# A list scheduler gets measured issue and landing times for transfers through DRAM

## The chip, the cores and the metric

The kernel runs on one NeuronCore of one Trainium2 chip. The metric is the device time of one execution in microseconds (us). A profile is one further execution, recorded by the hardware profiler; its span runs from its first to its last instruction. Engines are named as in the profile: PE (matmuls), PEld (weight loads), DVE (vector), ACT (scalar), POOL (GpSimd), SP (the engine that issues nearly all DMAs here).

## The reference, cut to what matters

Sixteen graphs (x is 16 x 1024 x 128) share one symmetric 0/1 adjacency matrix of 1024 x 1024. Layer 0 is an attention layer, layer 1 a gated graph network with five steps, and each is followed by a residual and a layernorm.

```python
h = x @ others_weight
e = leaky_relu(u1[:, idx1] + u2[:, idx2])        # u1 = h @ a1, u2 = h @ a2
att = softmax(where(adj > 0, e, NEG_BIG), axis=1)
x = layernorm(x + att @ h + x @ self_weight)
h = x
for _ in range(5):                               # per graph
    m = adj @ h                                  # in_matrix and out_matrix are both adj
    av = concat([m, m])
    u3 = h @ u3_w.T + u3_b
    z = sigmoid(av @ w3_w.T + w3_b + u3)
    r = sigmoid(av @ w4_w.T + w4_b + u3)
    hv = tanh(av @ w5_w.T + w5_b + (r * h) @ u5_w.T + u5_b)
    h = (1 - z) * h + z * hv
x = layernorm(x + h)
```

## The kernel before

One graph is called a batch b. Its state h lives turned, as hT (128 features x 1024 nodes), in two halves of 512 nodes. Per step s (`step`), PE makes m = adj @ h in two halves, each 16 matmuls at line 878: eight blocks of 128 nodes, each with a high and a low part of h (hN), since hN and adj are kept in fp32r. ACT copies each half out (line 896). Then per half: u from u3 (PE 908, ACT 911), the sums and gates r and z (PE 918, DVE 921, ACT 924), r times h (DVE 932), the candidate (PE 938 and 939, ACT 942), and three DVE operations that update hT (949, 956, 963). The gates' matmuls are plain fp32. For the next step h must be turned back, node by feature, and split into the high part (ACT cast, line 497) and the low part (DVE, line 501), together hN.

The turning is done by `flip` in most steps: a DVE transpose in blocks of 32 x 32 into tile T (line 478), then four DMA issues that write T to a DRAM tile D with blocks swapped (`away`, line 483), then one DMA issue that reads D back to tile F (line 487). Here it is called a flip. Layer 0 flips its result y and the normalised y (tiles T_y, D_y, F_y and T_b, D_b, F_b). `on_pe` makes the first two batches' layer-0 turns, and the last three batches' last step's, on PE instead (line 468, into PSUM). Layer 0 (`layer0`) also loads xt (line 516), and for b of 2 and more sends 24 rows (us) to DRAM as ud (line 573), from which come pb, spread over all partitions (line 580), and uu (line 587). A layernorm is bn_stats on DVE (441, 443), a power on POOL (447 to 450) and scaling on ACT (455). The result goes out at line 1006. Sixteen `look` loads of adj (line 1026) feed a late check.

The order of all this is not written by hand. Each operation is given to a planner, `Plan`, by `pe`, `dve`, `act`, `sp` and `plan.add`, with an engine, a length in ns, a rank (5b + 3s plus offsets from the table D; other spacings for the last two batches), and the values it reads and writes. `Plan.order` is a list scheduler: it runs a simulated clock, and whenever an engine is free it starts the ready operation of lowest rank whose tiles have a free buffer. Lengths on DVE and ACT are raised by 1.2. A user becomes ready at the end of the length plus a lag: LAG by the producer's engine, or SAME if the user is on the same engine:

```python
SAME = {"PE": 0, "DVE": 60, "ACT": 60, "POOL": 60, "SP": 2500, "DMA": 0}
LAG = {"PE": 250, "DVE": 150, "ACT": 170, "POOL": 200, "SP": 2500, "DMA": 2400}
```

So every DMA that SP issues was reckoned to land 2500 ns after its length. The order found is then emitted, and on the chip each engine's queue runs in that order[...]. An SP operation may hold several DMA issues: `away` has four, `uu_` two.

Of the kernel before, what the change touches and what calls it, by code (L numbers as in the profile page):

```python
# [30 lines left out]
class Plan:  # L31
# [11 lines left out]
    def __init__(self, slots):  # L43
        self.slots = dict(slots)
        self.ops = []
        self.writer, self.readers = {}, {}

    def add(self, engine, length, rank, emit, reads=(), writes=()):
        i = len(self.ops)
        deps = {self.writer[v] for v in reads if v in self.writer}  # L50
        for v in writes:
            deps |= self.readers.pop(v, set())
            if v in self.writer:
                deps.add(self.writer[v])
        for v in reads:
            self.readers.setdefault(v, set()).add(i)
        for v in writes:
            self.writer[v] = i
        deps.discard(i)
        tiles = {v[0] for v in (*reads, *writes) if v[0][0] in self.slots}  # L60
        if engine in ("DVE", "ACT"):
            length *= self.MARGIN
        self.ops.append((engine, length, rank, emit, deps, tiles))

    def order(self):
        ops, free = self.ops, dict(self.slots)
        users, left = [[] for _ in ops], []
        uses = {}
        for i, (_, _, _, _, deps, tiles) in enumerate(ops):
            left.append(len(deps))  # L70
            for d in deps:
                users[d].append(i)
            for t in tiles:
                uses[t] = uses.get(t, 0) + 1
        ready, busy, live = {}, {}, set()
        at = {}
        events = [(0, 0, i) for i in range(len(ops)) if not left[i]]
        heapq.heapify(events)
        started = []
        while events:  # L80
            now = events[0][0]
            while events and events[0][0] == now:
                _, what, i = heapq.heappop(events)
                engine, _, rank, _, _, tiles = ops[i]
                if what == 0:
                    heapq.heappush(ready.setdefault(engine, []), (rank, i))
                elif what == 1:
                    busy.pop(engine)
                    for t in tiles:
                        uses[t] -= 1  # L90
                        if not uses[t]:
                            free[t[0]] += 1
            more = True
            while more:
                more = False
                for engine, queue in ready.items():
                    if engine in busy:
                        continue
                    later = []
                    while queue:  # L100
                        rank, i = heapq.heappop(queue)
                        _, length, _, _, _, tiles = ops[i]
                        new = [t for t in tiles if t not in live]
                        if all(free[t[0]] > 0 for t in new):
                            for t in new:
                                free[t[0]] -= 1
                                live.add(t)
                            started.append(i)
                            busy[engine] = more = True
                            heapq.heappush(events, (now + length, 1, i))  # L110
                            for u in users[i]:
                                left[u] -= 1
                                lag = self.SAME[engine] if ops[u][0] == engine else self.LAG[engine]
                                at[u] = max(at.get(u, 0), now + length + lag)
                                if not left[u]:
                                    heapq.heappush(events, (at[u], 0, u))
                            break
                        later.append((rank, i))
                    for x in later:
                        heapq.heappush(queue, x)  # L120
        assert len(started) == len(ops)
        return started
# [3 lines left out]
def kernel(  # L126
# [52 lines left out]
    nc = tc.nc  # L179
# [26 lines left out]
    def exact(pools):  # L206
# [45 lines left out]
        def T(t, dtype=None, shape=None):  # L252
            if t not in tiles:
                _, sh, dt, _ = kinds[t[0]]
                tiles[t] = places[t[0]].tile(
                    shape or sh, dtype or dt, tag=t[0], name="_".join(map(str, t)).replace("-", "n")
                )
            return tiles[t]
# [25 lines left out]
        def sp(*a, **k):  # L284
            plan.add("SP", *a, **k)
# [31 lines left out]
        def early_loads():  # L317
# [28 lines left out]
            writes=[(boot, "early"), (ws, "early"), (x0, "early"), (("xt", 1), "early"), *((t, "early") for t in staged)],  # L346
# [125 lines left out]
        def flip(name, src, read, dst, write, rank):  # L472


            t, d = ("T", *name), ("D", *name)

            def turn():
                nc.vector.transpose(T(t).rearrange("p (b c i) -> p b c i", b=4, c=4), turned(src()))

            def away():  # L480
                swapped = T(d).rearrange("(b i) (a x) -> a i b x", b=4, a=4)
                for k in range(4):
                    nc.sync.dma_start(swapped[k], T(t)[32 * k : 32 * (k + 1), :].rearrange("i (b x) -> i b x", b=4))  # L483

            dve(V, rank, turn, reads=read, writes=[(t, 0)])
            sp(280, rank, away, reads=[(t, 0)], writes=[(d, 0)])
            sp(70, rank, lambda: nc.sync.dma_start(dst(), T(d)), reads=[(d, 0)], writes=[write])

        def split(b, s, g, src, read, rank):

# [16 lines left out]
        def layer0(b):  # L507

            first = rank_of(b, 0) - (60 if b == 0 else 0)
            rank = first + D["l1"]  # L510
            xt, hx, pb, u, us, uu, ud = (
                ("xt", b), ("hx", b), ("pb", b), ("u3", b), ("us", b), ("uu", b), ("ud", b)
            )
            q, zs, rz, yT, y0, hT = ("q", b), ("zs", b), ("rz", b), ("yT", b), ("y0", b), ("hT", b)
            if b >= 2:
                sp(2700, rank, lambda: nc.sync.dma_start(T(xt), x_t[b]), writes=[(xt, 0), (xt, 1)])

            for g in range(4):
                ph = ("ps", "g", b, "ph", g)
# [37 lines left out]
            if b >= 2:  # L557
# [6 lines left out]
                    reads=[(u, 0), (u, 1), (("ident",), 0)],  # L564
                    writes=[(put, 0)],
# [2 lines left out]
                    280, rank, lambda: nc.vector.tensor_copy(T(us), T(put)[0 : 3 * NC, 0:P]), reads=[(put, 0)], writes=[(us, 0)]  # L568
                )
                sp(  # L570
                    60,
                    rank,
                    lambda: nc.sync.dma_start(T(ud).rearrange("t (c p) -> (t c) p", p=P), T(us)),
                    reads=[(us, 0)],
                    writes=[(ud, 0)],
                )
                sp(
                    60,
                    rank,
                    lambda: nc.sync.dma_start(T(pb), T(ud)[2:3, :].to_broadcast([P, N])),  # L580
                    reads=[(ud, 0)],
                    writes=[(pb, 0), (pb, 1)],
                )

                def uu_():
                    for w in range(2):
                        nc.sync.dma_start(T(uu)[:, w, :], T(ud)[w].rearrange("(c p two) -> two p c", p=P, two=2)[w])

                sp(120, rank, uu_, reads=[(ud, 0)], writes=[(uu, 0)])

            else:

# [275 lines left out]
        def step(b, s):  # L868
# [99 lines left out]
            for g in range(2):  # L968
                gs = slice(4 * g, 4 * g + 4)
                o = ("o", b)  # L970

                def h(g=g):
                    return T(hT)[:, g * HALF : (g + 1) * HALF]

                if on_pe(b, s):
                    t = ("ps", "t", b, s, g)
                    transposes(h, [(hT, g)], t, rank + D["tr"])

                    def n(t=t):
                        return T(t).rearrange("p (c a j) -> p c a j", c=4, a=4)  # L980

                else:
                    t = ("F", b, s, g)
                    flip((b, s, g), h, [(hT, g)], lambda t=t: T(t), (t, 0), rank + D["tr"])

                    def n(t=t):
                        return chunks(T(t))

                if s < STEPS - 1:
                    split(b, s + 1, g, n, [(t, 0)], rank + D["split"])  # L990
                    continue

                def last(n=n, g=g, gs=gs):
                    dst = T(o)[:, gs, :].rearrange("p c (a j) -> p c a j", a=4)
                    nc.vector.tensor_tensor(dst, n(), T(y0)[:, gs, :].rearrange("p c (a j) -> p c a j", a=4), ALU.add)

                dve(V, rank + D["o"], last, reads=[(t, 0), (y0, g)], writes=[(o, "raw", g)])
                
                def at(j, g=g):
                    return T(o)[:, 4 * g + j, :]  # L1000

                layernorm(o, g, rank + D["ln"], (o, "raw", g), at, at, (o, g))
                sp(
                    60,
                    rank + D["out"],
                    lambda gs=gs: nc.sync.dma_start(
                        out[b].rearrange("(c p) d -> p c d", p=P)[:, gs, :], T(o)[:, gs, :]
                    ),
                    reads=[(o, g)],
                )  # L1010
# [332 lines left out]
```

## Time and profile before

| | us |
|---|---|
| three runs | 1522.34, 1528.13, 1528.56 (median 1528.13) |
| the profiled execution | 1530.39 |
| its span | 1528.60 |
| PE busy in it | 1497.9 (98%) |
| DVE, ACT, POOL busy | 1171.3, 841.6, 141.0 |
| mean granted PE clock | 0.993 |
| flips: D<-T, D_y<-T_y, D_b<-T_b issues | 616 + 112 + 112 |
| flips: F<-D, F_y<-D_y, F_b<-D_b issues | 154 + 28 + 28 |

The page gives, per engine, the time in which it was busy; per group of instructions, the mean of one and the idle time of the engine just before, with what ended it. An answer on waits reads "who <- for whom: us in total, times, longest". A timeline line reads: start, length, engine, line, operation, output <- input, shape, count, and in brackets the idle time before and what ended it. SP's own lines (SPq) are issues: what they show is the time in which SP was taken, not the movement of the data.

### The profile page before, as it was taken

The numbers are of one execution on the slowest core, as the hardware profiler recorded it, in microseconds if no ns is written. First come the engines' busy times: TensorE is split into PE (matmuls) and PEld (weight loads), VectorE is DVE, ScalarE is ACT, GpSimd is POOL, SyncE is SP. The second block draws the span as 40 slices with busy tenths as digits, with TensorE's granted clock in tenths as the row PEclk, the third lists the DMA queues.
The fourth block names the chain that finished last, engine by engine and source line by source line (L and its number), as shares of the span: only waits on it lengthen the run. The fifth ranks groups of instructions, "written<-read, shape, count | busy, mean of one in ns | idle before, by whom it ended". The sixth has DMA issues, their size and how long they took to land.

```text
span 1528.6 us, 17756 instructions
## 1 busy us (share of the span) xinstructions
PE 1497.9 (98%) x5200; PEld 944.5 (62%) x5200; DVE 1171.3 (77%) x2757; ACT 841.6 (55%) x1656; POOL 141.0 (9%) x265
## 2 busy tenths in 40 slices
PE   8999999999999999999999999999999999999996
PEld 7656566666666666666666566666666666666663
DVE  5778787878787777877878778777877888776665
ACT  4564645566465655555566455655555565555544
POOL 0101001011110201111011110101111011000001
PEclk9999999999999999999999999999999999999998
DMA  4124344242433324334242433324334233322121
GB/s 171 30 81 124 89 124 122 87 119 84 117 90 97 104 63 130 85 96 129 67 124 74 118 91 97 104 62 127 88 98 124 64 88 111 104 75 78 42 74 38
DMA packets 193982, 144.83 MB, mean 95 GB/s; under 512 B 33279, under 2 KB 158934, under 8 KB 193878
## 3 DMA queue, kind: packets, MB, share of 16 engines
q1 hardware_dynamic: 193314, 142.78, 32.8%
q8 instruction: 42, 0.69, 0.2%
q10 hardware_dynamic: 564, 0.85, 0.2%
q14 instruction: 62, 0.51, 0.1%
HBM read 79.95 MB, written 63.61 MB: 94 GB/s over the span
## 4 chain that ended last, share of the span: by engine, by line
PE 87%; DMA 4%; DVE 3%; POOL 2%; ACT 2%; SPq 1%; issue 1%; POOLq 0%; DVEq 0%; ACTq 0%
PE ps_acc L878 36%; PE ps_g_r L918 8%; PE ps_g_u L908 8%; PE ps_g_v L938 8%; PE ps_g_v L939 8%; PE ps_g_z L918 8%; PE ps_acc_po L749 7%; PE ps_g_ph L524 1%; DMA F<-D 1%; DMA D<-T 1%; SPq L483 1%; DMA F_y<-D_y 1%; POOL rstd_y L448 1%; PE ps_acc_po L805 1%; ACT y L455 1%
## 5 line engine op out<-in xcount | busy, mean ns | idle before, releaser
L878 PE MATMUL ps_acc<-adj,hN 128*128 128x512 f32 x2560 | 668.9, 415 | 0.7 <-DVE hN L501 0.7
L878 PEld LDWEIGHTS ps_acc<-adj,hN 128*128 128x128 f32 x2560 | 479.9, 188 | 166.9 <-issue 55.2
L896 ACT COPY m<-ps_acc 128x512 f32<-128x512 f32 x160 | 92.9, 580 | 156.7 <-PE ps_acc L878 156.4
L501 DVE TENSOR_TENSOR hN<-F,hN 128x512 fp32r<-128x512 f32 x128 | 88.1, 689 | 116.3 <-ACT hN L497 115.9
L942 ACT ACTIVATE hv<-ps_g_v,b 128x512 f32<-128x512 f32 x160 | 109.8, 687 | 105.5 <-PE ps_g_v L939 105.4
L918 PE MATMUL ps_g_r<-m,wm 128*128 128x512 f32 x320 | 164.4, 595 | 3.6 <-ACT m L896 3.6
L938 PE MATMUL ps_g_v<-m,wm 128*128 128x512 f32 x320 | 164.3, 595 | 3.4 <-ACT u L911 3.4
L939 PE MATMUL ps_g_v<-r,u5h 128*128 128x512 f32 x320 | 164.4, 595 | 0.3 <-DVE r L932 0.3
L918 PE MATMUL ps_g_z<-m,wm 128*128 128x512 f32 x320 | 163.4, 592 | 0.0
L497 ACT CAST hN<-F 128x512 fp32r<-128x512 f32 x128 | 79.1, 619 | 135.5 <-DMA F<-D 135.2
L921 DVE TENSOR_TENSOR r<-ps_g_r,u 128x512 f32<-128x512 f32 x160 | 109.0, 683 | 58.3 <-PE ps_g_r L918 55.0
L908 PE MATMUL ps_g_u<-hT,u 128*128 128x512 f32 x320 | 152.7, 598 | 0.7 <-ACT hT L861 0.7
L924 ACT ACTIVATE r<-r,bh 128x512 f32<-128x512 f32 x160 | 114.8, 721 | 67.5 <-DVE r L921 66.3
L949 DVE TENSOR_TENSOR hv<-hv,hT 128x512 f32<-128x512 f32 x160 | 109.5, 685 | 55.1 <-ACT hv L942 54.3
L749 PE MATMUL ps_acc_po<-adj,hl 128*128 128x512 f32 x512 | 145.5, 432 | 1.8 <-ACT hl L726 1.0
L749 PEld LDWEIGHTS ps_acc_po<-adj,hl 128*128 128x128 f32 x512 | 97.3, 190 | 42.1 <-issue 19.1
L924 ACT ACTIVATE z<-z,bh 128x512 f32<-128x512 f32 x160 | 113.0, 716 | 12.4 <-DVE z L921 11.6
L932 DVE SCALAR_TENSOR_TENSOR r<-r,hT 128x512 f32<-128x512 f32 x160 | 108.5, 681 | 12.7 <-ACT r L924 12.5
L911 ACT ACTIVATE u<-ps_g_u,bias 128x512 f32<-128x512 f32 x160 | 106.1, 682 | 17.5 <-PE ps_g_u L908 17.2
L956 DVE SCALAR_TENSOR_TENSOR hv<-z,hv 128x512 f32<-128x512 f32 x160 | 108.6, 680 | 3.4 <-ACT z L924 0.9
L921 DVE TENSOR_TENSOR z<-ps_g_z,u 128x512 f32<-128x512 f32 x160 | 108.5, 682 | 2.9 <-PE ps_g_z L918 2.0
L939 PEld LDWEIGHTS ps_g_v<-r,u5h 128*128 128x128 f32 x320 | 61.0, 191 | 77.7 <-issue 61.5
(132 smaller groups left out, 1482.5 us busy)
## 6 DMA issues: line engine op xcount, KB each, us to landing
D<-T SPq DMA_DIRECT2D x616, 64.0 KB
F<-D SPq DMA_DIRECT2D x154, 256.0 KB
out_dram<-o SPq DMA_DIRECT2D x32, 256.0 KB
xt<-in_x_dram SPq DMA_DIRECT2D x15, 512.0 KB
pb<-ud SPq DMA_DIRECT2D x14, 512.0 KB
D_y<-T_y SPq DMA_DIRECT2D x112, 64.0 KB
F_y<-D_y SPq DMA_DIRECT2D x28, 256.0 KB
D_b<-T_b SPq DMA_DIRECT2D x112, 64.0 KB
```

Of the source, the lines that this page charges most:

```text
L749: nc.tensor.matmul(T(po), hl[:, k, c, :], adj[:, c, hs], start=(first and i == 0), stop=(last and i == len(terms) - 1),)
L878: nc.tensor.matmul(T(pm), T(hN)[:, k, c, :], adj[:, c, hs[e]], start=(c == 0 and k == 0), stop=(c == NC - 1 and k == 1),)
L908: nc.tensor.matmul(T(pu), u3, h(), start=True, stop=True)
L918: nc.tensor.matmul(T(p_), wm[:, j, :], T(m), start=True, stop=True)
L921: nc.vector.tensor_tensor(T(t), T(p_), T(u), ALU.add)
L924: nc.scalar.activation(T(t), T(t), AF.Tanh, bias=bh[:, j : j + 1], scale=0.5)
L932: lambda r=r, h=h: nc.vector.scalar_tensor_tensor(T(r), T(r), 1.0, h(), ALU.add, ALU.mult),
L938: nc.tensor.matmul(T(pv), wm[:, 2, :], T(m), start=True, stop=False)
L939: nc.tensor.matmul(T(pv), u5h, T(r), start=False, stop=True)
L942: nc.scalar.activation(T(hv), T(pv), AF.Tanh, bias=b5, scale=1.0)
L949: lambda hv=hv, h=h: nc.vector.tensor_tensor(T(hv), T(hv), h(), ALU.subtract),
L956: lambda hv=hv, z=z: nc.vector.scalar_tensor_tensor(T(hv), T(z), 1.0, T(hv), ALU.add, ALU.mult),
```

## The change

The planner gets a `lag` per operation, and the SP operations get other lengths. What is computed, the instructions, the tiles and the ranks stay as they are; only the order that `Plan.order` finds may differ.

```diff
@@ class Plan
+        self.lag = {}
...
-    def add(self, engine, length, rank, emit, reads=(), writes=()):
+    def add(self, engine, length, rank, emit, reads=(), writes=(), lag=None):
         i = len(self.ops)
+        if lag is not None:
+            self.lag[i] = lag
...
                                 lag = self.SAME[engine] if ops[u][0] == engine else self.LAG[engine]
+                                lag = self.lag.get(i, lag)
                                 at[u] = max(at.get(u, 0), now + length + lag)
@@ flip
-            sp(280, rank, away, reads=[(t, 0)], writes=[(d, 0)])
-            sp(70, rank, lambda: nc.sync.dma_start(dst(), T(d)), reads=[(d, 0)], writes=[write])
+            sp(1830, rank, away, reads=[(t, 0)], writes=[(d, 0)], lag=1500)
+            sp(450, rank, lambda: nc.sync.dma_start(dst(), T(d)), reads=[(d, 0)], writes=[write], lag=2300)
@@ layer0: xt
-                sp(2700, rank, lambda: nc.sync.dma_start(T(xt), x_t[b]), writes=[(xt, 0), (xt, 1)])
+                sp(450, rank, lambda: nc.sync.dma_start(T(xt), x_t[b]), writes=[(xt, 0), (xt, 1)], lag=3500)
@@ layer0: ud, then pb
                 sp(
-                    60,
+                    450,
...
                 sp(
-                    60,
+                    450,
...
                     writes=[(pb, 0), (pb, 1)],
+                    lag=3000,
                 )
@@ layer0: uu
-                sp(120, rank, uu_, reads=[(ud, 0)], writes=[(uu, 0)])
+                sp(950, rank, uu_, reads=[(ud, 0)], writes=[(uu, 0)], lag=3000)
@@ step: the result's store
                 sp(
-                    60,
+                    450,
                     rank + D["out"],
```

The `look` loads keep their length of 60 and the lag of 2500.

## The prediction

> **What bounds the kernel now.** I read the page's first part, then the busy time by stretches, then the waits of PE, and last the timeline at those waits.
>
> ```profile
> PE 1497.9 (98%) x5200; PEld 944.5 (62%) x5200; DVE 1171.3 (77%) x2757; ACT 841.6 (55%) x1656; POOL 141.0 (9%) x265
> ```
>
> PE has work in all but 1528.60 - 1497.88 = 30.7 us of the span. A change of order makes no matmul shorter, so what it can win lies in these 30.7 us, and in stretches at a lower clock. The stretches say where (window in us, its length, then busy PE, PEld, DVE, ACT, POOL, then the granted clock):
>
> ```profile
> 60.00:90.00 30.00, 27.17 (x112) 17.89 (x111) 19.91 (x56) 13.82 (x30) 3.91 (x8) 1.00 0.31 89
> 150.00:165.00 15.00, 11.62 (x38) 6.16 (x37) 10.59 (x24) 8.69 (x17) 0.00 (x0) 0.89 0.57 160
> 340.00:1240.00 900.00, 896.41 (x3071) 563.24 (x3070) 706.44 (x1666) 507.95 (x1006) 89.87 (x160) 1.00 0.34 97
> 1240.00:1500.00 260.00, 260.00 (x855) 159.80 (x854) 187.36 (x371) 137.12 (x238) 15.42 (x32) 1.00 0.28 78
> 1500.00:1528.60 28.60, 13.51 (x51) 7.63 (x49) 14.86 (x49) 11.52 (x24) 7.37 (x16) 0.81 0.13 40
> ```
>
> PE is idle for 2.8 us at 60 to 90, 3.4 at 150 to 165, 3.6 in the long middle and 15.1 in the tail; the other 5.8 lie before 60 us (start-up loads). Start-up and tail don't depend on the changed costs: no transposition through DRAM is issued before 70 us, and the last three batches transpose their last step on PE. So 2.8 + 3.4 + 3.6 = 9.8 us can be reached. What ended the waits (times, longest):
>
> ```profile
> PE ps_g_r L918 <- ACT m L896: 3.6, 5, 1.2
> PE ps_t L468 <- DVE hT L963: 3.5, 2, 2.8
> PE ps_g_v L938 <- ACT u L911: 3.4, 1, 3.4
> PE ps_t_b L468 <- ACT y L455: 2.4, 3, 1.7
> ```
>
> All but the second (the tail) name ACT, which is only 55% busy. So ACT wasn't too slow; its work stood in the wrong order. At the longest:
>
> ```profile
> 153.53 0.62 ACT L497 CAST hN<-F 128x512 fp32r<-128x512 f32 x1 [2.94 <-DMA F<-D]
> 154.05 1.33 ACT L924 ACTIVATE r<-r,bh 128x512 f32<-128x512 f32 x2
> 156.17 0.62 ACT L497 CAST hN<-F 128x512 fp32r<-128x512 f32 x1 [0.78 <-DMA F<-D]
> 156.69 1.33 ACT L924 ACTIVATE z<-z,bh 128x512 f32<-128x512 f32 x2
> 157.93 1.24 ACT L911 ACTIVATE u<-ps_g_u,bias 128x512 f32<-128x512 f32 x2
> 158.65 1.62 PE L938 MATMUL ps_g_v<-m,wm 128*128 128x512 f32 x2 [3.38 <-ACT u L911]
> ```
>
> ACT stood 2.94 + 0.78 us at two casts whose data (F) came late; the gates r and z and the additions u, queued behind, were late, and PE with them. Over the run ACT waits for F<-D at L497 for 135.2 us in 88 of 128 casts. Mostly PE has other batches' work meanwhile; at the start it hasn't.
>
> [...] The stretch 150:165 agrees: clock 0.89, so 15 x 0.114 = 1.7 us of PE time are lost besides the idle 3.4. [...] The trace agrees: a D<-T issue takes SP 0.43 us, and the data has landed 1.75 us after the issue began (chain of waits at 333.44).
>
> **The change part by part.** No instruction is added or removed; the planner gets other costs and writes other queues. (1) A flip (DVE turn, four D<-T issues, one F<-D issue). The old plan books, from the turn's end to F's readers, 0.15 + 0.28 + 2.50 + 0.07 + 2.50 = 5.50 us; the new one 0.15 + 1.83 + 1.50 + 0.45 + 2.30 = 6.23, and SP is taken for 2.28 us of it, not 0.35. In the trace I matched each of the 210 turns to its four issues, its F<-D and its first reader in queue order: turn's end to reader is 5.68 us at least, 7.6 in the median. The four issues take 1.84 (median). So the new plan foresees 0.73 us more, plus SP's queueing, which in the trace is 0.6 us in the mean ahead of the first issue: some 1.3 of the 2.1 us by which the old one is short. (2) SP's share. The new plan books 14 x 2.28 + xt 0.45 + ud 0.45 + pb 0.45 + uu 0.95 + two outs 0.90 = 35 us per batch, which takes some 91.6 us on PE: 38%. SP isn't the bound, but in bursts its queue is now ordered by rank, so a step's D<-T can stand behind four D_b<-T_b issues (1.8 us). (3) xt: 0.45 + 3.50 instead of 2.70 + 2.50, so 1.25 us sooner, and SP isn't held; free, as it is loaded long ahead except for the first at 72 us. (4) ud, pb, uu, out: 0.4 to 0.8 us more on SP each, pb and uu land 0.9 and 1.3 us later than booked before. The trace shows SP issues of 0.33 to 0.44 there; hidden behind some 50 us of other batches' PE work. Later readers of F and uu move back on ACT and DVE, and nothing on PE's side needs them then, except in the two-batch end (below).
>
> The sum, against the profiled run of 1530.39 us (span 1528.60, 1.8 around it). **Long stall at 155:** 3.38 + 1.7 = 5.1, taken as gone: ACT would do r, z and u before the casts. What is late next is hv of the same step, with PE's next group ready. **Start, 60 to 90:** of 1.67 us at ps_t_b, up to 1.6 go if y's scaling goes ahead of a cast (the cast held ACT for 2.27 us); I take half, 0.8, since a POOL chain ends just behind. The rest there (xt 0.45, hN 0.65 behind pb) stays. **Middle:** 3.6 us in five waits, each a second layernorm scaling ahead of m, as here:
>
> ```profile
> 501.13 1.65 ACT L455 ACTIVATE y<-F_y,rstd_y 128x128 f32<-128x128 f32 x4 [0.70 <-POOL rstd_y L450]
> 502.68 0.56 ACT L896 COPY m<-ps_acc 128x512 f32<-128x512 f32 x1
> ```
>
> With F_y foreseen later I take half as gone, 1.8. Together 7.7. **New waits:** the plan stays short by 0.8 us in the median, and under load F takes 3.9 us where 2.75 are booked. New order opens new waits: at half the middle's rate, 3.6/900 x 1430 x 0.5 = 2.9, and one of 1.2 us (the longest of the middle) at the start: 4.1. Bounds for this unknown: 0 and about 11. Net 7.7 - 4.1 = 3.6: 1526.8, and since the profiled run is 2.3 above the median of 1528.13, **1524.5 us**.
>
> **The rivals.** *All waits go:* 5.1 + 2.8 + 3.6 = 11.5, none new: 1516.7. For it: all are waits of order; against: landings vary more than any plan knows. *No change at PE:* PE is 98% busy, three batches interleave, and casts moved later on an ACT that is half idle cost and win nothing; the long stall only changes its place: 1528. That the change hardly alters the order belongs here. *Slower, by the two-batch end:* from about 1314 to 1500 us only the last two batches alternate, and PE, now without any gap, gets hN just before it needs it:
>
> ```profile
> 1462.62 0.69 DVE L501 TENSOR_TENSOR hN<-F,hN 128x512 fp32r<-128x512 f32 x1 [0.77 <-ACT hN L497]
> 1464.09 1.27 PE L878 MATMUL ps_acc<-adj,hN 128*128 128x512 f32 x3
> ```
>
> That is 1464.09 - 1463.31 = 0.8 us to spare (3.2 at 1430). If the new queues put one block of D<-T issues (1.84 us) ahead of a step's F<-D there, each of some 11 steps waits 1.0 us: 11.4, and two waits that also cost the clock 3.4. Less the 3.6 of above: 1524.5 + 14.8 = 1539. It decides from 0.8 us of lateness. Against it: the new plan books the real issue time, so it sees this wait and can order around it.
>
> **How the numbers follow.** Net gain as summed 0.46 (own range 1520 to 1529), no change 0.26, all waits gone 0.14, two-batch end 0.14. About 0.5%, 7.6 us, is what a measurement of this kernel can tell from no change (its three runs span 6.2 us). Below 1520.5: the 0.14, and 0.13 of the likeliest: 0.27. Above 1535.8: most of the last, 0.12. Between: 0.61. The range 1516 to 1536 leaves out the outer ends of the second and fourth.
>
> **What would show it.** Right: ACT's wait at L497 for F<-D well under 135 us; no PE gap over 2 us between 90 and 1500; no half clock after 60 us; PE idle in the middle under 3.6 us. Wrong: PE waits for hN (L501) or ps_t after 1314; SP's four-issue blocks ahead of an F<-D that PE needs; a repeating gap in each batch; a longer start before 165 us.

## The result, and the profile after

| | before | changed |
|---|---|---|
| median of 7 runs (lowest to highest), us | 1526.5 (1522.34 to 1528.56) | 1517.85 (1515.81 to 1519.17) |
| the profiled execution, its span | 1530.39, 1528.60 | 1515.81, 1514.00 |

The ratio is 0.9947, 95% interval 0.9931 to 0.9963: the change takes 8.65 us off the median. The forecast was 1524.5 us with a gain of 3.6. The time lies within the full range (1516 to 1536), but below the likeliest case's own (1520 to 1529); what came is close to the rival in which all waits go (1516.7), to which the prediction gave 0.14. By the gain it lies between the two (3.6 and 11.5 us), since more runs have put the median of before at 1526.5 instead of 1528.13.

The changed kernel's page, its first part:

```profile
PE 1491.3 (99%) x5200; PEld 944.2 (62%) x5200; DVE 1167.0 (77%) x2757; ACT 843.7 (56%) x1656; POOL 142.2 (9%) x265
```

The instructions are the same ones: 5200, 2757, 1656 and 265 as before. PE is idle for 1514.0 - 1491.3 = 22.7 us instead of 30.7, and its own busy time is 6.6 us less. Of these 6.6, 3.4 are clock: ahead of the tail the profile of before has three half-clock windows (from 26.0, 46.5 and 159.1 us), this one has one (from 45.0 us), each of 3.41 us at a granted clock of 0.5, so that each costs 1.7 us. Some 2.3 more, an estimate, lie beside the waits: a matmul ahead of a wait counts in full (0.59 us, where otherwise the next one starts 0.43 us after it), and PE has 16 waits instead of 30. Its busy time by stretches (columns as before):

```profile
60.00:90.00 30.00, 29.02 (x118) 18.99 (x116) 21.73 (x61) 15.43 (x33) 3.40 (x8) 1.00 0.32 89
150.00:165.00 15.00, 15.00 (x59) 10.73 (x58) 12.48 (x29) 7.26 (x17) 0.00 (x0) 1.00 0.57 158
340.00:1240.00 900.00, 900.00 (x3087) 567.42 (x3086) 712.01 (x1684) 515.33 (x1018) 89.14 (x156) 1.00 0.34 97
1240.00:1500.00 260.00, 257.39 (x847) 157.29 (x845) 183.47 (x368) 137.92 (x238) 18.68 (x40) 1.00 0.26 76
```

The 15 us from 150 are full and at full clock, and so is the whole middle. The 2.6 us missing in the last line are the tail, which now begins before 1500. What PE still waits for:

```profile
PE ps_t L472 <- DVE hT L968: 3.5, 2, 2.7
PE ps_t_b L472 <- ACT y L459: 1.5, 1, 1.5
```

The first is the tail, as before. The second lies at 43 us, ahead of the first flip. ACT's waits for data from DRAM, before and then changed:

```profile
ACT hN L497 <- DMA F<-D: 135.2, 88, 5.0
```

```profile
ACT hN L501 <- DMA F<-D: 60.5, 52, 3.5
```

135.2 us in 88 waits have become 60.5 in 52. The transfers are no quicker. Matching each of the 210 flips again, the time from turn to reader is 8.0 us in the median (7.6 before), and from the turn's end to the end of the F<-D issue 4.5 (4.7 before). The readers come later, but ACT seldom stands at them.

The two profiles differ by 14.6 us, more than the medians do: the profiled run of before lay 3.9 us above its median, that of the changed kernel 2.0 under.

### The profile page after: what moved, and what is told of

The parts are those of the page before. It is cut to its first block, busy times and chain, and to the rows that moved or that the text cites. A ratio compares the mean times of both kernels' runs of the same rounds, so it can differ in the third digit from the quotient of the medians.

```text
span 1514.0 us, 17727 instructions
## 1 busy us (share of the span) xinstructions
PE 1491.3 (99%) x5200; PEld 944.2 (62%) x5200; DVE 1167.0 (77%) x2757; ACT 843.7 (56%) x1656; POOL 142.2 (9%) x265
## 4 chain that ended last, share of the span: by engine, by line
PE 96%; DVE 1%; ACT 1%; POOL 1%; DMA 0%; issue 0%; SPq 0%; POOLq 0%
PE ps_acc L883 39%; PE ps_g_u L913 9%; PE ps_g_r L923 9%; PE ps_g_z L923 9%; PE ps_g_v L944 9%; PE ps_g_v L943 9%; PE ps_acc_po L754 8%; PE ps_g_ph L528 2%; PE ps_acc_po L810 1%; PE ps_acc_px L796 1%; DMA hN_boot<-in_adj_dram 0%; ACT y L459 0%; POOL rstd_y L452 0%; PE ps_idle L400 0%; DVE junk L683 0%
## 5 line engine op out<-in xcount | busy, mean ns | idle before, releaser
L943 PE MATMUL ps_g_v<-m,wm 128*128 128x512 f32 x320 | 163.3, 592 | 0.0
L501 ACT CAST hN<-F 128x512 fp32r<-128x512 f32 x128 | 78.8, 616 | 60.9 <-DMA F<-D 60.5
```

The lines of the kernel that those rows point to most:

```text
L943: nc.tensor.matmul(T(pv), wm[:, 2, :], T(m), start=True, stop=False)
```

## Where the start comes right

In the queues that the planner wrote, the change does more at the start than I had argued. DVE, before, from 129 us:

```profile
130.30 0.69 DVE L501 TENSOR_TENSOR hN<-F,hN 128x512 fp32r<-128x512 f32 x1 [3.09 <-ACT hN L497]
132.70 0.43 DVE L1033 TENSOR_SCALAR junk_look<-look 128x512 f32<-128x512 f32 x1 [1.70 <-DMA look<-in_adj_dram]
...
137.98 0.70 DVE L478 STREAM_TRANSPOSE T_y<-yT 128x512 f32<-128x512 f32 x1
```

DVE stood 3.09 us at a low part whose cast was waiting for F, then 1.70 at a `look`; what had piled up behind was worked off from 132.70 on. So batch 2's second half of y, copied out by ACT at 131.33 to 131.92, was turned only at 137.98, 6.1 us later. ACT and then DVE in the changed kernel:

```profile
127.22 0.58 ACT L825 COPY yT<-ps_acc_po 128x512 f32<-128x512 f32 x1 [4.00 <-PE ps_acc_po L754]
```

```profile
128.69 0.70 DVE L482 STREAM_TRANSPOSE T_y<-yT 128x512 f32<-128x512 f32 x1
```

Here the turn follows 0.9 us after the copy. Batch 2 is further on, and in the changed plan its first sum m comes early enough to be used. This is PE's queue in the two plans, places 131 to 136 (batch, step, half; m is the sum adj @ h, r a gate):

```
     before                     changed
131  h of batch 4 (ph 3)        1 1 0 candidate
132  batch 4 px                 1 1 1 candidate
133  1 1 0 candidate            2 0 0 m
134  1 1 1 candidate            0 3 0 m
135  0 3 0 m                    0 3 1 m
136  0 3 1 m                    0 3 0 r
```

One sum of batch 2 now stands between batch 1's candidate and batch 0's sum, whose hN comes late. PE and ACT of the changed kernel there:

```profile
152.59 1.02 PE L944 MATMUL ps_g_v<-r,u5h 128*128 128x512 f32 x2
153.05 8.26 PE L883 MATMUL ps_acc<-adj,hN 128*128 128x512 f32 x33
```

```profile
149.55 0.72 ACT L929 ACTIVATE z<-z,bh 128x512 f32<-128x512 f32 x1
150.18 0.67 ACT L916 ACTIVATE u<-ps_g_u,bias 128x512 f32<-128x512 f32 x1
...
155.44 0.62 ACT L501 CAST hN<-F 128x512 fp32r<-128x512 f32 x1 [2.55 <-DMA F<-D]
```

ACT waits 2.55 us for F here too, but with r, z and u done; PE runs on without a gap. Whether ACT's order alone is enough, an experiment below asks (one_flip).

## The experiments

Theories: *foresight* (mine): the flips' booked time makes the gain, since late readers are put behind other work. Rivals: *occupancy* (SP's booked issue time counts, the landing doesn't), *other loads* (xt, pb, uu, stores), and *shuffle* (any new order loses one unlucky wait). Each ratio is to runs of before taken alongside, whose median was 1527.99 us for the first four experiments, 1526.44 for the next four and 1526.34 for one_flip and flip_long.

**flip_only and rest_only: which costs.** flip_only is the change with these five put back (in short form):

```diff
-sp(450, rank, ... T(xt), x_t[b] ..., lag=3500)
+sp(2700, rank, ... T(xt), x_t[b] ...)
-450 (ud), 450 and lag=3000 (pb), 950 and lag=3000 (uu), 450 (store)
+60 (ud), 60 (pb), 120 (uu), 60 (store)
```

> Only the flips get the new lengths and lags; xt, ud, pb, uu and the stores keep the old ones. Foresight theory (the gain comes from the flips being booked 6.23 us instead of 5.50, so that casts and layernorm scalings stand behind the gates on ACT): ratio to before 0.994 to 0.996, ACT's wait for F<-D near 60 us, no PE gap over 2 us between 90 and 1490 us. If the other loads carry the gain: 0.998 to 1.002. Shuffle theory (any new order loses the one unlucky wait at 155 us): 0.994 to 0.998, whatever ACT's wait is.

rest_only is the change with the flips put back:

```diff
-sp(1830, rank, away, ..., lag=1500)
-sp(450, rank, ... T(d) ..., lag=2300)
+sp(280, rank, away, ..., lag=2500)
+sp(70, rank, ... T(d) ..., lag=2500)
```

> The flips keep the old lengths and lags; xt, ud, pb, uu and the stores get the new ones. Foresight theory: ratio 0.998 to 1.002, ACT's wait for F<-D stays near 135 us, waits of PE on ACT of the same kind, though perhaps at other places. Shuffle theory: 0.994 to 0.998 with ACT's wait for F<-D near 135 us.

flip_only: 1516.53 us, ratio 0.9925 (0.9911 to 0.9939), better than the theory had it. ACT waits for F<-D 34.1 us, PE has no gap from 90 to 1490. rest_only: 1529.5, ratio 1.0013 (1.0005 to 1.0021). ACT waits 138.6 us, and PE's longest wait is there again, on another operation of ACT:

```profile
PE ps_g_v L943 <- ACT hv L947: 4.4, 1, 4.4
PE ps_t_b L472 <- ACT y L459: 3.2, 2, 1.7
PE ps_t L472 <- DVE hT L968: 3.1, 2, 2.8
PE ps_g_r L923 <- ACT m L901: 2.8, 3, 2.0
```

Its order differs from that of before on every queue but POOL's, so shuffle falls (time_only, late_new and one_flip below are new orders without a gain, too), and other loads with it: the flips carry the gain. The other loads' new costs do both good and harm at the start. Where xt has its new costs PE waits 1.5 us at 42 us, with the old ones 0.2 + 0.5. From 60 to 90 us it is the other way about: PE is idle for 3.6 us in flip_only, 1.9 of it in one wait with a half-clock window behind it, and for 1.0 us in the changed kernel. The wait, with a shorter one at 46 us:

```profile
PE ps_g_u L912 <- ACT hT L865: 2.6, 2, 1.9
```

Whether flip_only is quicker than the change, the overlapping intervals don't say.

**time_only and busy_only: landing or occupancy.** The flips in time_only (the total of 6.23 us kept), then in busy_only (the old total of 5.50):

```diff
+sp(280, rank, away, ..., lag=3050)
+sp(70, rank, ... T(d) ..., lag=2680)
```

```diff
+sp(1830, rank, away, ..., lag=950)
+sp(450, rank, ... T(d) ..., lag=2120)
```

> All as in the change, but SP is booked as taken for the old 0.28 and 0.07 us per flip, and the lags are raised so that the flip's total stays 6.23 us (3.05 and 2.68). Foresight theory by latency alone: ratio 0.994 to 0.996, ACT's wait for F<-D 60 to 80 us. Theory that SP's occupancy is what counts (its queueing foreseen, its queue ordered by rank in bursts): 0.998 to 1.000, ACT's wait over 100 us.

> All as in the change, with SP booked as taken for 1.83 and 0.45 us per flip, but the lags cut (0.95 and 2.12) so that the total of an undisturbed flip is the old 5.50 us. Latency theory: ratio 0.997 to 1.000, ACT's wait for F<-D 100 to 135 us. Occupancy theory: 0.994 to 0.996, ACT's wait 60 to 80 us.

time_only: 1527.16, ratio 0.9996 (0.9988 to 1.0004), ACT's wait 107.4 us; the long wait of PE stays:

```profile
157.62 2.08 PE L943 MATMUL ps_g_v<-m,wm 128*128 128x512 f32 x2 [3.52 <-ACT u L916]
```

busy_only: 1520.51, ratio 0.9955 (0.9942 to 0.9968), ACT's wait 89.9 us (60 to 80 were expected), one gap of 0.91 us left at 152. So 0.73 us more of landing alone win nothing; the time in which SP is taken wins most of it. My sum had led with the 0.73 us and put the queueing behind it.

**late_flat and longer: enough foresight of another kind, and more of it.** late_flat keeps SP's old occupancy and books the landings very late; longer adds to the change's lags:

```diff
+sp(280, rank, away, ..., lag=4300)
+sp(70, rank, ... T(d) ..., lag=3350)
```

```diff
+sp(1830, rank, away, ..., lag=2000)
+sp(450, rank, ... T(d) ..., lag=3300)
```

> SP booked as taken for the old 0.28 and 0.07 us per flip, but landings booked so late (lags 4.30 and 3.35) that a flip's total is 8.15 us, above the 7.6 us seen in the median. Theory that foresight of any kind is enough (readers stand far enough back on ACT): the long wait at 150 to 160 us is gone, ACT's wait for F<-D under 60 us, ratio to before 0.993 to 0.996. Theory that SP's occupancy itself must be booked (its bursts ordered and stretched in the plan): a wait of 2 us or more remains at 150 to 160, ratio 0.998 to 1.000.

> SP's occupancy as in the change, lags raised to 2.00 and 3.30, so a flip's total is 7.73 us. If what the change leaves of ACT's waits (60 us for F<-D) still costs PE: ratio 0.991 to 0.994. If PE is bound by its own work from 90 us on: as the change, 0.993 to 0.996, with ACT's wait under 40 us. If overbooking makes hN late in the two-batch end: waits of PE for hN after 1300 us and 0.996 to 1.000.

late_flat: 1519.53, ratio 0.9961 (0.9947 to 0.9975), no gap at 150 to 165, ACT's wait 9.2 us, one gap of 1.1 us at 138. So occupancy isn't needed as such: 8.15 us booked flatly do it, 6.23 don't, and 5.50 with SP's queueing reckoned nearly do. longer: 1517.21, ratio 0.9942 (0.9925 to 0.9959), ACT's wait 6.5 us. Compared with the change, 54 us less waiting on ACT bring nothing that shows: from 90 us to the tail PE is bound by its own work. No wait for hN came up in the two-batch end, even with 1.5 us more booked.

**start_new and late_new: where.** The flips' new costs for some batches, all else as in the change:

```diff
+new = name[0] < 3          # late_new: name[0] >= 3
+sp(1830 if new else 280, rank, away, ..., lag=1500 if new else 2500)
+sp(450 if new else 70, rank, ... T(d) ..., lag=2300 if new else 2500)
```

> New lengths and lags for the flips of batches 0 to 2 only; later batches' flips keep the old ones, all else as in the change. By the ledger of the two profiles the start (60 to 165 us, with its half clock) holds 7 us and the middle 3.6: ratio 0.995 to 0.997, the long wait gone, waits of PE on ACT's m left in the middle. If the middle holds the gain: 0.998 to 1.000.

> New lengths and lags for the flips of batches 3 and later only; batches 0 to 2 keep the old ones, all else as in the change. By the ledger: ratio 0.997 to 0.999, a wait of 2 us or more left at 150 to 160, no wait of PE on ACT's m in the middle. If the middle holds the gain: 0.994 to 0.996.

start_new: 1520.11, ratio 0.9962 (0.9948 to 0.9976); no gap at 150, and in the middle only three of 0.3 us and one of 0.1, though the flips there have the old costs and ACT waits 108.4 us. late_new: 1528.0, ratio 1.0008 (0.9999 to 1.0017), where 0.997 to 0.999 was expected; gaps of 2.0 and 2.5 us at 152 to 165, and one of 2.2 at 358. So three of sixteen batches make most of the gain; whether the others add to it, the overlapping intervals of start_new and the change don't say. The middle's waits, too, seem to follow from how the start leaves the batches to one another: they nearly go with the start's costs alone, and late_new, with the middle's own costs new, still has one.

**one_flip: the cast alone.** All costs of before, but for the flip whose casts held ACT:

```diff
-sp(70, rank, ... T(d) ...)
+sp(70, rank, ... T(d) ..., lag=5400 if name[:2] == (0, 2) else 2500)
```

> All lengths and lags as before the change, but for one step's flip: batch 0, step 2, the one whose two casts held ACT at 153 to 157 us; its two F<-D are booked to land 2.90 us later, so that a flip's total there is 8.40 us, as the trace shows (8.36). PE's queue keeps 984 of 996 places. Theory that this one misplaced pair of casts makes most of the gain: the gap at 155 us and the half clock at 159 us are gone, ratio to before 0.996 to 0.998. Theory that the gain is spread over the order, or comes from the middle: 0.999 to 1.001, or a gap of the same size at another place of the start.

1526.79, ratio 1.0002 (0.9991 to 1.0013). Both casts moved behind r and z of batch 1 on ACT, as meant. PE in this kernel:

```profile
157.09 1.02 PE L943 MATMUL ps_g_v<-r,u5h 128*128 128x512 f32 x2
157.78 0.57 PE L882 MATMUL ps_acc<-adj,hN 128*128 128x512 f32 x1
160.58 0.74 PE L882 MATMUL ps_acc<-adj,hN 128*128 128x512 f32 x2 [2.23 <-DVE hN L505]
```

The candidate (L942 and L943) is no longer late, but the next group in PE's queue is batch 0's own sum, and the low part of its hN isn't there. It isn't F that is late now. ACT and DVE:

```profile
155.35 0.62 ACT L501 CAST hN<-F 128x512 fp32r<-128x512 f32 x1 [1.24 <-DMA F<-D]
```

```profile
159.15 0.16 DVE L659 TENSOR_TENSOR seen<-uu 128x4 f32<-128x4 f32 x1 [5.30 <-DMA uu<-ud]
159.83 0.69 DVE L505 TENSOR_TENSOR hN<-F,hN 128x512 fp32r<-128x512 f32 x1
```

Both casts were done by 155.97 us. The low part stood on DVE behind an operation that waited 5.30 us for uu, another load through DRAM, which still had its old costs here; before, the low part stood ahead of it. The wait has moved by some 3 us, with a half-clock window behind it (granted clock 0.90 from 150 to 165 us), and 4.2 us of gaps are left between 165 and 1240 us. Both expectations miss part of it: the old wait is gone, the gain isn't. What one_flip would gain with uu out of the way was not tried.

**flip_long: a candidate for better.** flip_only with the lags of longer:

```diff
+sp(1830, rank, away, ..., lag=2000)
+sp(450, rank, ... T(d) ..., lag=3300)
```

> New lengths for the flips with lags 2.00 and 3.30 (total 7.73 us), old ones for xt, ud, pb, uu and the stores. A candidate for better than the change: if the other loads' new costs lose something, 0.990 to 0.993; if PE is bound by its own work from 90 us on, as the change, 0.993 to 0.996.

1517.2, ratio 0.9935 (0.9916 to 0.9953): not to be told from the change. PE has no gap from 82 to 1495 us. It is also another order: its plan keeps batch 2's sum behind batch 0's, as before, but puts batch 0's candidate ahead of batch 1's sum, so that the flip starts sooner. The planner has more than one way to fill the delay; in the changed kernel, too, the first half's turn ends at 141.78 us instead of 145.17.

**What the plans foresee.** That first half's flip of batch 0, step 2, took 8.4 us before the change (turn's end 145.17, cast 153.53). `Plan.order`, run on each kernel, books from turn to landing: 5.77 us in before, rest_only and late_new, 6.23 in time_only, 6.38 in busy_only, 6.56 in the change and in start_new, 7.33 in flip_only, 8.50 in flip_long, 8.87 in late_flat and 9.52 in longer. Up to 6.23 us there is no gain, from 6.38 on there is; one_flip (8.67), where uu came in between, is the exception. So the gain goes with more foresight, but comes well short of the true delay. Why 6.38 us turn the order and 6.23 don't is not shown.

**before_again and after_again.** Both kernels once more:

> The kernel before, profiled once more. If the wait at 155 us is one of order and not of chance, it stands there again with 2.5 to 4.5 us and half a clock window behind it; the number of half-clock windows before 60 us may differ (the start's gaps there are the same instructions), and the span with it by 1.7 us for each.

> The changed kernel, profiled once more. If its order holds against scatter of landings: no PE gap over 1 us from 60 to 1490 us; half-clock windows before 60 us one or two, not the same number as in the first profile of need.

before_again (1528.52):

```profile
0.00:60.00 60.00, 54.88 (x294) 41.51 (x295) 40.70 (x150) 35.44 (x95) 5.95 (x17) 1.00 0.32 109
60.00:90.00 30.00, 27.61 (x109) 18.60 (x108) 19.97 (x60) 13.44 (x31) 3.42 (x8) 0.94 0.30 89
90.00:150.00 60.00, 60.00 (x202) 37.46 (x201) 49.86 (x117) 30.70 (x60) 4.57 (x8) 1.00 0.37 105
150.00:165.00 15.00, 11.52 (x42) 6.94 (x41) 10.66 (x24) 9.28 (x19) 0.00 (x0) 0.89 0.52 143
```

The wait at 155 stands again, 15.00 - 11.52 = 3.5 us with a half-clock window (granted clock 0.89, so 15 x 0.11 = 1.7 us). It belongs to the order. The windows ahead of it come and go: none before 60 us and one at 78 us (0.94) here, two before 60 us and no other in the first profile of before. after_again (1515.91) has no gap over 0.8 us from 60 to 1490, and two such windows before 60 us where the first had one.

## Why the prediction was right, by its own steps

The range held; the reckoning behind it held in part. The sum names 3.6 us of gain, 8.65 were measured, and that the range took this in is owed to the rival with all waits gone. The signs named for being right did come: ACT's wait for F<-D at 60.5 us, no idle time in the middle, and from 60 us to the tail no half clock and no gap of PE over 0.8 us. The steps one by one:

- *The long stall, 5.1 us:* gone, with its half clock. That it would go because ACT does r, z and u before the casts was half the reason. "With PE's next group ready" had no reason of its own: in one_flip ACT has that order, and PE then waits 2.23 us for the next group, which DVE's queue holds up. In the changed kernel a sum of batch 2 stands there, in flip_long the flip is started sooner. PE, DVE and ACT had to come right together.
- *Start, 60 to 90, 0.8 us:* taken too small, it was 29.02 - 27.17 = 1.85.
- *Middle, half of 3.6 us:* all of it went. That F_y is foreseen later there, as I had it, isn't needed: start_new leaves the middle's flips as before and still has only 1.1 us of gaps.
- *New waits, 4.1 us:* the step that failed most: between 90 and 1490 us the two profiles of the changed kernel have 0.08 us and none. Half the middle's old rate of waits was a guess without a run behind it. What was lost is about 0.8 us at 43 us, where xt's new costs put ph ahead of the transpositions (1.52 us of waiting instead of 0.21 + 0.54); I had called xt free.
- *The sum:* 5.1 + 1.85 + 3.6 - 0.8 = 9.75 us by the two profiles, 8.65 between the medians; forecast 3.6. The profiles themselves differ by 14.6: no term named the half-clock window before 60 us (1.7 us, and chance) and the time beside the waits.
- *Foresight of 0.73 us plus 0.6 of queueing:* the plans foresee 5.74 us for a flip in the mean before and 6.78 after, so 1.0 and not 1.3, since the old plan had some queueing too; and in the median the new plan stays short by 1.4 us (6.56 booked, 8.0 taken), not by 0.8. The weights were wrong, as time_only and busy_only show.
- *The two-batch end as a loss:* it didn't come. PE is full from 1240 to the tail, and longer shows no wait there either.

Open: which queue of the changed plan is indispensable. One queue of the one plan with the other queues of the other can't be run: by the operations' dependencies PE's, DVE's, ACT's and SP's queues would then wait for each other in a circle, whichever are mixed.

## What to carry to other kernels

A list scheduler should book a transfer nearer to what it takes when several stand in the issuing queue than to what one takes alone (a flip took 5.68 us at least before the change, 7.6 in the median): occupancy of the issuer plus landing, or a flat value of the loaded case. Booking longer cost nothing that shows here (7.73 us against 6.23), booking too short cost the start. Book every load that shares a queue, or the wait may move to the next, as it did to uu (5.30 us in one_flip). And look for the gain where few batches are in flight: in start_new ACT waits 108.4 us for F<-D and PE loses 1.1 us of it between 90 and 1490 us at most, while three batches at the start decide.

## What the runs showed of the hardware

Half-clock windows stood behind short waits of PE, too. Of nine waits of PE of 1.9 to 2.5 us between 60 and 1490 us (in before_again, flip_only, rest_only, time_only, late_new and one_flip) six came with one; of the four of 3.4 to 4.4 us (before, before_again, rest_only, time_only) all did. From 150 to 165 us the granted clock was 0.89 with a wait of 3.4, 3.5 and 4.4 us (before, before_again, rest_only), 0.90 with one of 2.2 (one_flip), and 1.00 in the changed kernel, without a wait. Each of the four windows ahead of the tail in the profiles of before and of the changed kernel lasted 3.41 us at a granted clock of 0.5 and so cost 1.7 us; by that estimate a wait of 2 us with a window behind it cost up to 3.7. What sets a window off is not shown.

ACT kept to the order of its queue: before the change DVE had the sums for both r done at 149.13 and 150.84 us, and ACT was idle from 150.59 to 153.53, but r began at 154.05, behind the cast that waited for F.

One issue took SP longer than the others: the F<-D issue at 149.36 us, before, took 1.70 us, where the median of the 154 is 0.34 and the next longest 0.42. What held it is not shown.
